# Cross-attention with four key sets on one core: keys copied at the slot's opening, last output and value products interleaved, a new end

## The chip, the core and the metric

The kernel runs on one core of one Trainium2 chip, written for that core's engines: TensorE (PE in the profile; its weight loads are listed apart as PEld), VectorE (DVE), ScalarE (ACT), GpSimd (POOL) and SyncE (SP), which here only issues DMAs. Each engine runs its own instructions in order and waits on semaphores for what other engines or DMAs produce. The metric is the device time of one execution in microseconds, median of several runs.

## The reference

The inputs `x` (32 x 512 x 640) and `ctx` (32 x 77 x 1024) are float32. For each of the 32 batches:

```python
q = heads(x @ to_q_w)                       # 20 heads of 32
k, v = heads(ctx @ to_k_w), heads(ctx @ to_v_w)
p = softmax(q @ k.T / sqrt(32))             # 512 x 77 per head
out = merge(p @ v) @ to_out_w + to_out_b + x
```

The source has four key sets (text, object, others, image prompt), but the context has exactly the 77 text tokens, so the other three sets are empty and add nothing.

## The kernel before, in words

All products are made in a float32 split: an operand is held as a rounded high part (type fp32r, written by ACT) and the remainder as a low part (written by DVE or POOL), and each product is three matmuls, high x high, high x low, low x high (`PAIRS`).

**Key and value phase (about the first 270 us).** The 2464 context rows are five groups of 512 (the last 416). For a group, `context` transposes the context on DVE (L167) and splits it (L103 on ACT, L104 on DVE); `keys` and `values_of_chunk` multiply it by the key and value weights on PE (L191, tiles `pk` and `pv`); `split_keys` and `split_values` split the results and write them to DRAM (`k_dram`, `v_dram`). `split_values` begins with a DVE transpose (L228) into one of two buffers `vs`, which must wait until the DMAs that read that buffer have landed. At the end of group 0 the order on DVE and ACT is: value split 2, key split 3, value split 3, context pieces 1 and 2 of the next group, key split 4, context pieces 3 to 7, value split 4. At the end of group 3 it is value split 3, then context pieces 1 to 7 of group 4, then value split 4.

**Slots.** After that the program is 160 slots, `slot(n)` with `b, j = divmod(n, 5)`: one batch and one of its five chunks of four heads. A slot's work is a pipeline over several slots, written out by hand, and the order of the calls is the order on each engine:

- queries of the next slot: 15 matmuls (L444, `pq<-xt,wq_s`), in two parts of 6 and 9; `split_q` copies and splits them (ACT L455, POOL L459, DVE L461).
- scores of this slot in four parts of 128 rows: 3 matmuls each (L479, `sc<-kb,qt`), into one of three PSUM buffers; DVE takes the row maxima (L487, `nm`) and ACT the exponentials (L497, `pn`, with row sums).
- probabilities of the slot before: reciprocal (DVE L507), multiplication (POOL L512, `normalize`), transposition (DVE L519, tile `z`) and four DMAs to DRAM (L526). They are loaded again (L535, L536, tile `raw`) and used four slots after their scores (`LAG`).
- probabilities taken now: `cast_p` (ACT L543) writes the high part, `rest_p` the last rows' high part (ACT L549) and the low part (DVE L550), `last_p` the last rows' low part (POOL L557).
- `values`: 6 matmuls (L571, `pa<-pp,vb`). `sum_a` adds the two halves (ACT L582, DVE L584), and in the next slot's opening `high_a` and `low_a` split the sum into `at` (ACT L591, DVE L596). `pa` has one buffer, so the next `values` waits for both.
- output product, `piece`: 24 matmuls per slot (L614, `po<-wo_s,at`), of one or two batches before; `finish` adds bias and residual (DVE L643) and stores. At j = 4 the first piece is 2 x 3 matmuls that need the `at` of the chunk just split.
- keys: `kb0` holds chunks 0 to 2 of a batch, `kb1` chunks 3 and 4. SP loads them (L420), at j = 3 for the next batch's `kb0` and at j = 0 for `kb1`, and `copy_keys` (POOL L424, L425) copies them into two further planes. It stands after `split_q` and `add_bias` of the slots j = 1 (`kb1`) and j = 4 (`kb0`), and the scores of the next slot, j = 0, read `kb0`.
- x of the next batch but one is loaded, transposed on DVE (L257, `TRANSPOSE_X` says in which of three places of which slot), and split (ACT L264, POOL L265) in slots j = 2 and 3.
- `add_bias` (POOL L607) adds the bias to the residual.

Slots 0 to 7 have no output product yet. `end()` takes the last four slots' probabilities and makes the remaining output products.

SP issues all DMAs of the slots in order, and a DMA waits until the one eight before it has landed.

The lines that the change moves most:

```python
            split_q(n + 1)
            if bias_now:
                add_bias(b - BIAS[j][0], BIAS[j][1])
            if j == 1:
                copy_keys(1)
            elif j == 4:
                copy_keys(0)
            exps(n, 2, *s)
```

Of the kernel before, what the change touches and what calls it, by code (L numbers as in the profile page):

```python
# [8 lines left out]
F32 = mybir.dt.float32  # L9
# [14 lines left out]
P = 128  # L24
# [27 lines left out]
def kernel(  # L52
# [278 lines left out]
    for g in range(LAST):  # L331
        for j in range(NC_):
            if g or j > 2:
                values_of(g, j, psk)
            if not g and j < 3:
                split_keys(0, j)
            if not g and j == 2:
                continue
            if j == 1:
                context(g + 1, 0)  # L340
            if not g and j == 3:
                split_values(0, 2)
                split_keys(0, 3)
            if j == NC_ - 1:
                if not g:
                    context(g + 1, 1, 2)
                    split_keys(0, 4)
                context(g + 1, *range(1 if g else 3, NK))
                if g + 1 == LAST:
                    kvw.release()  # L350
                    kvc.release()
                    xpool.append(
                        ctx.enter_context(
                            tc.tile_pool(name="xpool", bufs=1, reuse_waits="tile")
                        )
                    )
                    load_x(0)
            split_values(g, j, (None, split_wq, split_wo, None)[g])
# [180 lines left out]
    def cast_p(n):  # L539

        raw = raws[n]
        pp = late[0].tile([P, 5, S], FPR, tag="pp", name="pp", bufs=1)
        nc.scalar.copy(pp[:, 0:2, :], raw[:, 0:2, :])  # L543
        pps[n] = pp

    def rest_p(n):

        raw, pp = raws[n], pps[n]
        nc.scalar.copy(pp[:64, 4, :], raw[:64, 2, :])  # L549
        nc.vector.tensor_tensor(  # L550
            pp[:, 2:4, :], raw[:, 0:2, :], pp[:, 0:2, :].bitcast(F32), ALU.subtract
        )
# [9 lines left out]

    PASSES = [(p, 0, p + c) for p in range(2) for c in (0, 2)] + [(p, 1, 4) for p in range(2)]

    def values(n):
        b, j = divmod(n, NC_)
        g = GROUP_OF[j]
        pp, vb = pps.pop(n), vbs[g][:, j - GROUPS[g][0]]
        pas[n] = late[1].tile([P, 2, S], F32, tag="pa", name="pa", bufs=1)
        for m, (p, t, c) in enumerate(PASSES):  # L570
            nc.tensor.matmul(  # L571
# [39 lines left out]

    def project(b, t, h, j):
        for m, (a, c) in enumerate(PAIRS):
            nc.tensor.matmul(  # L614
# [4 lines left out]
                stop=(j == NC_ - 1 and m == 2),  # L619
            )  # L620


# [37 lines left out]
    BIAS = {2: (1, 0), 4: (1, 1), 0: (2, 2), 1: (2, 3)}  # L660
    TRANSPOSE_X = {0: ((), (), (0,)), 1: ((), (1,), (2,)), 2: ((3,), (), ())}
    SPLIT_X = {2: ((0,), (1,)), 3: ((2, 3), (4,))}
# [25 lines left out]
    def slot(n, beside=()):  # L688
# [9 lines left out]
        if not filling:  # L698
            refill(b, j, 0)
        if taken is not None:  # L700
            cast_p(taken)
# [39 lines left out]
        if not ahead:  # L741
            exps(n, 2, *s)
            piece(bo_, first)
            finish()
            s = scores(n, 3)
        early = ahead and has_out and j in (1, 4)
        if early:
            piece(bo_, first)
            finish()
        if not ahead:  # L750
            transpose_p(n - 1)
        if ahead:
            split_q(n + 1)
            if bias_now:
                add_bias(b - BIAS[j][0], BIAS[j][1])
            if j == 1:
                copy_keys(1)
            elif j == 4:
                copy_keys(0)
            exps(n, 2, *s)  # L760
        if n and not has_out:
            transpose_p(n - 1)
        if j == 4 and b + 2 < B:
# [3 lines left out]
        if not ahead:  # L767
            exps(n, 3, *s)
            normalize(n, sums(n))
            finish()  # L770
            piece(bo_, first + 1)
            values(taken)
            sum_a(taken)
# [4 lines left out]
        else:  # L778
            s = scores(n, 3)
        if taken is not None:  # L780
            values(taken)
# [20 lines left out]
    def end():  # L802
# [6 lines left out]
        piece(last - 1, 4)  # L809
        finish()  # L810
        high_a(N - 5)
        cast_p(N - 4)
        low_a(N - 5)
        rest_p(N - 4)
        last_p(N - 4)
        add_bias(last - 1, 2)
        piece(last - 1, 5)
        transpose_p(N - 1)
        add_bias(last - 1, 3)
        load_p(N - 2)  # L820
        piece(last - 1, 6)
        finish()
        take(N - 4)
        piece(last - 1, 7)
        cast_p(N - 3)
        rest_p(N - 3)
        last_p(N - 3)
        finish()
        load_p(N - 1)
        load_residual(last, 0)  # L830
        load_residual(last, 1)
        piece(last - 1, 8)
        take(N - 3)
        piece(last - 1, 9)
        cast_p(N - 2)
        rest_p(N - 2)
        last_p(N - 2)
        finish()
# [19 lines left out]

        begin(0, 0, 2)
        begin(1, 0, 2)  # L860
        take(N - 2)
        cast_p(N - 1)
        rest_p(N - 1)
        last_p(N - 1)
        for t in (0, 1, 3, 2):
            add_bias(last, t)
        begin(2, 0, 3)
        begin(0, 2, 4)
        begin(1, 2, 4)
        begin(2, 3, 4)  # L870
        begin(3, 0, 4)
        take(N - 1)
        begin(4, 0, 4)
        begin(5, 0, 4)

# [78 lines left out]
```

## Time and profile before

| | |
|---|---|
| median of 3 runs | 2061.75 us (2060.82 to 2064.63) |
| profiled execution, its own time | 2063.8 us |
| span of its instructions | 2062.0 us |
| TensorE busy | 1938.3 us, 94% |
| VectorE, ScalarE, GpSimd busy | 1571.7, 1551.5, 1368.4 us |
| mean granted TensorE clock | 0.981 |
| DMA | 431 MB, mean 209 GB/s |

The page gives for each engine the busy time and instructions, then the span in slices, the DMA queues, the chain of work that ended last, and the costliest groups of instructions by source line, with the idle time of the engine before them and what ended it. A matmul's end is modelled and overlaps the next one's start, so what a group of matmuls costs is read from start to start. Times in the trace's views are from the span's start. The clock is shown as a share: 1.00 is full, 0.50 half.

The slots are regular. From the start of one slot's first scores to the next one's, slots j = 0 to 4 take about 10.1, 9.9, 10.3, 10.2 and 13.4 us; the slot j = 0 takes 11.7 us in 13 of the batches.

### The profile page before, as it was taken

To read this page: it belongs to the slowest core of one execution; us is meant where nothing else is said; L and a number is where in the kernel's file an instruction comes from. 1 tells how busy PE (TensorE), PEld (TensorE's weight loads), DVE (VectorE), ACT (ScalarE), POOL (GpSimd) and SP (SyncE) were. 2 spreads that over 40 slices of the span, in tenths; PEclk is the share of its full clock that TensorE was granted. 3 is DMA by queue.
4 is the path that set the end of the run, shared out by engine and by line. 5 is a ranking of instruction groups with operands and counts; after the bars stand their busy time and mean duration, and the time that the engine had idled before them with its cause. 6 is when DMAs were issued, how large, how long until landed. Compare 5 with 4: busy or idle time off the path is not lost.

```text
span 2062.0 us, 37523 instructions
## 1 busy us (share of the span) xinstructions
PE 1938.3 (94%) x10332; PEld 1690.2 (82%) x10332; DVE 1571.7 (76%) x2494; ACT 1551.5 (75%) x6210; POOL 1368.4 (66%) x1116
## 2 busy tenths in 40 slices
PE   9999997999999999999999999999999999999997
PEld 7787886888888888888888888888888888888887
DVE  4344457888888888888888888888888888888874
ACT  3232258888888888888888888888888888888872
POOL 1000166777777777877777777777777777877763
PEclk9999998999999999999999999999999999999999
DMA  9878778888888888878788888878788888888774
GB/s 194 199 180 229 178 187 222 218 217 221 208 214 219 207 218 217 221 208 222 198 215 211 218 209 210 223 214 224 206 219 212 214 219 210 219 216 211 202 198 143
DMA packets 565023, 431.37 MB, mean 209 GB/s; under 512 B 191120, under 2 KB 473168, under 8 KB 564816
## 3 DMA queue, kind: packets, MB, share of 16 engines
q1 hardware_dynamic: 560304, 414.47, 79.2%
q0 software_dynamic: 4416, 14.34, 2.1%
q8 instruction: 85, 1.39, 0.3%
q14 instruction: 122, 1.00, 0.2%
q10 hardware_dynamic: 96, 0.16, 0.0%
HBM read 247.17 MB, written 181.64 MB: 208 GB/s over the span
## 4 chain that ended last, share of the span: by engine, by line
DVE 35%; PE 17%; issue 14%; ACT 12%; DMA 9%; POOL 6%; SPq 6%; DVEq 0%; POOLq 0%; ACTq 0%
DVE z L519 8%; ACT pn L497 7%; DVE nm L487 5%; PE pq L444 5%; DVE pp L550 5%; DVE qt L461 5%; DMA raw<-pd 4%; DVE pa L584 3%; DVE xs L257 3%; PE po L614 3%; DMA xs<-in_x_dram 3%; PE sc L479 2%; DVE at L596 2%; PE pk L191 2%; PE pv L191 2%
## 5 line engine op out<-in xcount | busy, mean ns | idle before, releaser
L497 ACT ACTIVATE pn<-sc,nm 128x77 f32<-128x77 f32 x2560 | 802.7, 334 | 137.4 <-DVE nm L487 130.3
L614 PE MATMUL po<-wo_s,at 128*128 128x320 f32 x3840 | 641.0, 315 | 35.2 <-DVE at L596 28.4
L444 PE MATMUL pq<-xt,wq_s 128*128 128x512 f32 x2400 | 647.6, 410 | 3.5 <-POOL xt L265 0.3
L614 PEld LDWEIGHTS po<-wo_s,at 128*128 128x128 f32 x3840 | 571.8, 190 | 46.1 <-DVE at L596 37.1
L557 POOL TENSOR_TENSOR pp<-raw,pp 64x512 fp32r<-64x512 f32 x160 | 304.6, 1904 | 369.3 <-ACT pp L549 301.2
L497 ACT ACTIVATION_READ_ACCUMULATOR pn<-sc,nm 128x1 f32 x2560 | 541.5, 212 | 0.0
L444 PEld LDWEIGHTS pq<-xt,wq_s 128*128 128x128 f32 x2400 | 438.5, 195 | 93.5 <-POOL xt L265 16.6
L479 PEld LDWEIGHTS sc<-kb,qt 128*128 128x128 f32 x1920 | 337.4, 192 | 133.5 <-POOL kb L425 62.3
L479 PE MATMUL sc<-kb,qt 128*128 128x154 f32 (+1 forms) x1920 | 342.1, 281 | 66.4 <-POOL kb L425 48.7
L487 DVE TENSOR_REDUCE nm<-sc 128x4 f32<-128x308 f32 x640 | 291.5, 464 | 136.5 <-PE sc L479 132.3
L512 POOL TENSOR_TENSOR pn<-pn,rs 128x1232 f32<-128x1232 f32 x160 | 364.2, 2277 | 14.2 <-DVE rs L507 1.8
L461 DVE TENSOR_TENSOR qt<-pq,qt 64x512 fp32r<-64x512 f32 x320 | 220.2, 688 | 122.6 <-ACT qt L455 117.6
L571 PE MATMUL pa<-pp,vb 128*128 128x512 f32 x960 | 256.5, 402 | 5.2 <-DVE at L596 2.4
L519 DVE STREAM_TRANSPOSE z<-pn 128x1280 f32<-128x1280 f32 x160 | 241.8, 1512 | 6.1 <-POOL pn L512 0.8
L584 DVE TENSOR_TENSOR pa<-pa,aw 64x512 f32<-64x512 f32 x320 | 222.7, 696 | 28.1 <-ACT aw L582 17.7
L550 DVE TENSOR_TENSOR pp<-raw,pp 128x1024 fp32r<-128x1024 f32 x160 | 202.5, 1266 | 29.7 <-ACT pp L543 29.7
L265 POOL TENSOR_TENSOR xt<-xs,xt 128x512 fp32r<-128x512 f32 x160 | 202.6, 1292 | 33.6 <-ACT xt L264 30.8
L459 POOL CAST qt<-qt 64x512 fp32r<-64x512 f32 x320 | 195.4, 611 | 33.1 <-ACT qt L455 14.3
L582 ACT COPY aw<-pa 64x1024 f32<-64x1024 f32 x160 | 162.0, 1013 | 65.9 <-PE pa L571 62.9
L571 PEld LDWEIGHTS pa<-pp,vb 128*128 128x128 f32 x960 | 173.8, 189 | 43.3 <-DVE at L596 11.9
L607 POOL TENSOR_TENSOR xr<-xr,bias 128x640 f32<-128x640 f32 x128 | 200.7, 1569 | 12.2 <-PE sc L479 2.0
L543 ACT CAST pp<-raw 128x1024 fp32r<-128x1024 f32 x160 | 168.9, 1056 | 1.8 <-DMA raw<-pd 1.8
(46 smaller groups left out, 1566.6 us busy)
## 6 DMA issues: line engine op xcount, KB each, us to landing
pd<-z SPq DMA_DIRECT2D x640, 160.0 KB, 3.2
raw<-pd SPq DMA_DIRECT2D x160, 512.0 KB, 4.1
xs<-in_x_dram SPq DMA_DIRECT2D x128, 320.0 KB, 7.4
xr<-in_x_dram SPq DMA_DIRECT2D x128, 320.0 KB, 3.3
out_dram<-xr SPq DMA_DIRECT2D x127, 320.0 KB, 3.6
raw<-pd SPq DMA_DIRECT2D x160, 128.0 KB, 4.2
v_dram<-vs SPq DMA_DIRECT2D x80, 192.0 KB, 3.9
k_dram<-ks POOLq DMA_DIRECT2D x20, 512.0 KB, 3.2
```

Of the source, the lines that this page charges most:

```text
L444: nc.tensor.matmul(pqs[n], wq_s[:, k, a, j * P : (j + 1) * P], xts[b, k][:, c, :], start=(k == 0 and m == 0), stop=(k == NC_ - 1 and m == 2),)
L461: nc.vector.tensor_tensor(qt[r, 1 + w, :], pq[r], qt[r, 0, :].bitcast(F32), ALU.subtract)
L479: nc.tensor.matmul(sc[:, cols], qt[:, m, t * P : (t + 1) * P], keys_, start=(m == 0), stop=(m == 2),)
L487: nc.vector.tensor_reduce(nm, sc[:, :KCOLS].rearrange("p (h k) -> p h k", k=NKEY), AX.X, ALU.max, negate=True)
L497: nc.scalar.activation(pnb[n % 2][:, at, :NKEY], sc[:, i * NKEY : (i + 1) * NKEY], AF.Exp, bias=nm[:, i : i + 1], accum_out=sms[n][:, at : ...
L512: nc.gpsimd.tensor_tensor(pf, pf, rs.unsqueeze(2).to_broadcast([P, NQ * HPC, NKEY]), ALU.mult)
L519: nc.vector.transpose(z.rearrange("p b t j -> p t b j"), pn.rearrange("p (t h) k -> p t (h k)", t=NQ).rearrange("p t (b i) -> p t b i", i=Q),)
L550: nc.vector.tensor_tensor(pp[:, 2:4, :], raw[:, 0:2, :], pp[:, 0:2, :].bitcast(F32), ALU.subtract)
L557: nc.gpsimd.tensor_tensor(pp[64:, 4, :], raw[:64, 2, :], pp[:64, 4, :].bitcast(F32), ALU.subtract)
L571: nc.tensor.matmul(pas[n][:, p, :], vb[:, p, t, :], pp[:, c, :], start=(c == p), stop=(t == 1),)
L584: nc.vector.tensor_tensor(pa[64 * p : 64 * p + 64, 0], pa[:64, p], aw[:, p], ALU.add)
L614: nc.tensor.matmul(pos[b, t, h][:, :HALF], ats[b * NC_ + j][:, a, t * P : (t + 1) * P], wos[0][:, j, c, h * HALF : (h + 1) * HALF], start= ...
```

## The change

- `split_values` of chunk 3 in the key and value phase stands after context pieces 1 and 2 of the next group.
- `copy_keys` stands at the opening of the slots j = 1 and j = 4, ahead of `cast_p`.
- The copy of the probabilities' last rows (ACT L549) moves from `rest_p` into `cast_p`: it runs ahead of `high_a`.
- `values` makes its six products in another order (both halves' first product, then both second, then both third) and can be made in two parts. `close_first`, at j = 4, replaces the first piece and `values`: 2 x 2 output matmuls that need only the high part of `at`, four of the values' matmuls, 2 x 1 output matmuls that need the low part, the last two of the values' matmuls.
- One transposition of x in slot j = 1 moves from behind the slot's third scores to behind its second exponentials.
- In the slots without output, the transposition of the probabilities stands behind the fourth scores.
- `end()` has a new order: in each step `turn` sums and splits one slot's values alternately with the cast of the next one's probabilities, and the output products of the last batch are made in layers (chunks 0 and 1 of four tiles, then chunk 2, then chunk 3).

The same amount of every kind of instruction is executed, apart from the last slots' order.

```diff
             if not g and j == 3:
                 split_values(0, 2)
                 split_keys(0, 3)
+            if j == 3:
+                continue
             if j == NC_ - 1:
+                context(g + 1, 1, 2)
                 if not g:
-                    context(g + 1, 1, 2)
                     split_keys(0, 4)
-                context(g + 1, *range(1 if g else 3, NK))
+                split_values(g, 3, (None, split_wq, split_wo, None)[g])
+                context(g + 1, *range(3, NK))
...
         nc.scalar.copy(pp[:, 0:2, :], raw[:, 0:2, :])
+        nc.scalar.copy(pp[:64, 4, :], raw[:64, 2, :])
         pps[n] = pp
 
     def rest_p(n):
 
         raw, pp = raws[n], pps[n]
-        nc.scalar.copy(pp[:64, 4, :], raw[:64, 2, :])
...
-    PASSES = [(p, 0, p + c) for p in range(2) for c in (0, 2)] + [(p, 1, 4) for p in range(2)]
+    PASSES = [(p, 0, p + c) for c in (0, 2) for p in range(2)] + [(p, 1, 4) for p in range(2)]
...
+    def close_first(b, n):
+
+        for m0, m1, v0, v1 in ((0, 2, 0, 4), (2, 3, 4, 6)):
+            for h in range(2):
+                project(b, 0, h, NC_ - 1, m0, m1)
+            values(n, v0, v1)
+        closed.extend(((b, 0, 0), (b, 0, 1)))
...
-    TRANSPOSE_X = {0: ((), (), (0,)), 1: ((), (1,), (2,)), 2: ((3,), (), ())}
+    TRANSPOSE_X = {0: ((), (), (0,)), 1: ((1,), (), (2,)), 2: ((3,), (), ())}
...
         if not filling:
             refill(b, j, 0)
+        if j == 1:
+            copy_keys(1)
+        elif j == 4 and more:
+            copy_keys(0)
         if taken is not None:
             cast_p(taken)
...
         if early:
-            piece(bo_, first)
+            if j == 4:
+                close_first(bo_, taken)
+            else:
+                piece(bo_, first)
             finish()
...
-            if j == 1:
-                copy_keys(1)
-            elif j == 4:
-                copy_keys(0)
             exps(n, 2, *s)
-        if n and not has_out:
-            transpose_p(n - 1)
...
         else:
             s = scores(n, 3)
-        if taken is not None:
+            if n:
+                transpose_p(n - 1)
+        if taken is not None and not (early and j == 4):
             values(taken)
...
+        def turn(n):
+            sum_a(n)
+            cast_p(n + 1)
+            high_a(n)
+            rest_p(n + 1)
+            low_a(n)
+            last_p(n + 1)
...
-        begin(0, 0, 2)
-        begin(1, 0, 2)
-        take(N - 2)
-        cast_p(N - 1)
-        rest_p(N - 1)
-        last_p(N - 1)
+        for i in range(4):
+            begin(i, 0, 2)
+        values(N - 2)
+        turn(N - 2)
         for t in (0, 1, 3, 2):
             add_bias(last, t)
-        begin(2, 0, 3)
-        begin(0, 2, 4)
-        begin(1, 2, 4)
-        begin(2, 3, 4)
-        begin(3, 0, 4)
+        for i in range(4):
+            begin(i, 2, 3)
+        for i in (4, 5):
+            begin(i, 0, 3)
         take(N - 1)
-        begin(4, 0, 4)
-        begin(5, 0, 4)
+        for i in range(6):
+            begin(i, 3, 4)
```

More of the change, by code (lines that the diff above doesn't have):

```diff
@@ L559, in last_p, with values @@
         )
-    PASSES = [(p, 0, p + c) for p in range(2) for c in (0, 2)] + [(p, 1, 4) for p in range(2)]
-    def values(n):
+    PASSES = [(p, 0, p + c) for c in (0, 2) for p in range(2)] + [(p, 1, 4) for p in range(2)]
+    def values(n, m0=0, m1=6):
         b, j = divmod(n, NC_)
         g = GROUP_OF[j]
-        pp, vb = pps.pop(n), vbs[g][:, j - GROUPS[g][0]]
-        pas[n] = late[1].tile([P, 2, S], F32, tag="pa", name="pa", bufs=1)
-        for m, (p, t, c) in enumerate(PASSES):
+        pp, vb = pps[n], vbs[g][:, j - GROUPS[g][0]]
+        if m1 == 6:
+            pps.pop(n)
+        if m0 == 0:
+            pas[n] = late[1].tile([P, 2, S], F32, tag="pa", name="pa", bufs=1)
+        for p, t, c in PASSES[m0:m1]:
             nc.tensor.matmul(
@@ L610, in output_bank, with project @@
         pos[b, t, h] = late[1].tile([P, S], F32, tag="po", name="po", bufs=2)
-    def project(b, t, h, j):
-        for m, (a, c) in enumerate(PAIRS):
+    def project(b, t, h, j, m0=0, m1=3):
+        for m in range(m0, m1):
+            a, c = PAIRS[m]
             nc.tensor.matmul(
@@ L747, in slot @@
         if early:
-            piece(bo_, first)
+            if j == 4:
+                close_first(bo_, taken)
+            else:
+                piece(bo_, first)
             finish()
@@ L769, in slot @@
             normalize(n, sums(n))
+            piece(bo_, first + 1)
             finish()
-            piece(bo_, first + 1)
-            values(taken)
             sum_a(taken)
@@ L810, in end @@
         finish()
+        cast_p(N - 4)
         high_a(N - 5)
-        cast_p(N - 4)
+        rest_p(N - 4)
+        transpose_p(N - 1)
         low_a(N - 5)
-        rest_p(N - 4)
         last_p(N - 4)
         add_bias(last - 1, 2)
-        piece(last - 1, 5)
-        transpose_p(N - 1)
         add_bias(last - 1, 3)
         load_p(N - 2)
+        piece(last - 1, 5)
         piece(last - 1, 6)
         finish()
-        take(N - 4)
+        values(N - 4)
         piece(last - 1, 7)
-        cast_p(N - 3)
-        rest_p(N - 3)
-        last_p(N - 3)
         finish()
+        def turn(n):
[5 more added lines that the diff above has]
+            last_p(n + 1)
+        turn(N - 4)
         load_p(N - 1)
@@ L832, in end @@
         piece(last - 1, 8)
-        take(N - 3)
+        finish()
+        values(N - 3)
         piece(last - 1, 9)
-        cast_p(N - 2)
-        rest_p(N - 2)
-        last_p(N - 2)
+        turn(N - 3)
         finish()
```

## The prediction

> **What bounds the kernel now.** First the page: PE is busy 94% of the span, so the time is PE's work plus its waits. Then PE's waits by releaser, which name three places the change touches.
>
> ```profile
> PE 1938.3 (94%) x10332; PEld 1690.2 (82%) x10332; DVE 1571.7 (76%) x2494; ACT 1551.5 (75%) x6210; POOL 1368.4 (66%) x1116
> ```
>
> ```profile
> PE sc L479 <- POOL kb L425: 48.7, 29, 3.4
> PE po L614 <- DVE at L596: 28.4, 33, 1.1
> PE pk L191 <- ACT ct L103: 6.2, 2, 3.2
> ```
>
> Third, the timeline, for the end of a slot j = 4: PE waits 0.92 us for the low part of `at`, and 1.66 us at the next slot's first scores for POOL's key copies, which stand behind the bias addition.
>
> ```profile
> 1187.07 0.85 PE L614 MATMUL po<-wo_s,at 128*128 128x320 f32 x4 [0.92 <-DVE at L596]
> ...
> 1193.99 0.97 PE L479 MATMUL sc<-kb,qt 128*128 128x308 f32 x3 [1.66 <-POOL kb L425]
> 1194.76 2.85 PE L444 MATMUL pq<-xt,wq_s 128*128 128x512 f32 x6
> ```
>
> ```profile
> 1191.22 1.56 POOL L607 TENSOR_TENSOR xr<-xr,bias 128x640 f32<-128x640 f32 x1
> 1192.74 0.56 POOL L424 CAST kb<-kb 64x462 fp32r<-64x462 f32 x1
> 1193.36 0.57 POOL L425 CAST kb<-kb 64x462 fp32r<-64x462 f32 x1
> ```
>
> Fourth, stretches: after such a wait the granted clock (PEclk, behind POOL's count) is 0.50, so six matmuls take 2.85 us instead of 1.59. A slot j = 4 is 13.45 us with PE busy 10.76, one j = 1 is 9.86 us without idle time; DMA is full in j = 4 (share 1.02).
>
> ```profile
> 1194.60:1197.40 2.80, 2.80 (x7) 2.23 (x8) 2.32 (x4) 2.08 (x10) 1.98 (x1) 0.50 1.12 318
> ```
>
> ```profile
> 1126.63:1140.08 13.45, 10.76 (x59) 8.81 (x58) 11.66 (x18) 13.01 (x50) 11.53 (x11) 1.00 1.02 232
> ...
> 1150.19:1160.05 9.86, 9.86 (x59) 8.93 (x58) 8.60 (x16) 8.09 (x34) 6.05 (x5) 1.00 0.75 194
> ```
>
> Last, the chain of waits. It doesn't run through PE here, but from transposition to transposition through DVE and ACT without a gap: this is what comes next once PE's waits go.
>
> ```profile
> 1312.54 1.50 DVE z L519
> ...
> 1319.23 1.34 ACT pn L497 x8
> 1320.57 0.48 ACT qt L455
> ...
> 1321.08 0.69 DVE qt L461
> ...
> 1324.54 0.73 DVE xs L257
> ...
> 1344.35 1.52 DVE z L519
> ```
>
> **The steady part.** From the opening of slot 9 (361.7 us) to that of slot 154 (1945.1) are 29 batches, 54.60 us each. Five slots at the 9.85 of j = 1 make 49.25, the floor on PE. But each batch must also pass the DVE and ACT chain. In the batch at 1127 us, `z` starts at 1127.02 (j = 3), 1137.33, 1149.10, 1159.59, 1170.83, 1180.92: steps of 10.31, 11.77, 10.49, 11.24, 10.09, in sum 53.90. DVE waited for scores in the second, 0.57 and 1.72 us, and only there. Without these the chain needs 53.90 - 2.29 = 51.61. So of PE's 5.35 us over its floor, some 3 can go before this chain binds.
>
> *Copies at the opening.* With the copies ahead, the first scores of j = 0 start right behind the output product: 1.66 us of wait go, and with them the slow clock, 3.41 us at half speed = 1.7 us, in 12 of the 29 batches. This ends DVE's two waits: counted from the end of L596 in j = 4 (1133.11), PE would need 4.8 us to the scores (4 values 0.93, 2 po 0.30, 2 values 0.47, scores 0.33, 18 po 2.70) and reach the fourth scores of j = 0 at about 1145.7 instead of 1148.1, when DVE, 0.57 earlier, is ready at 1146.3. What is queued behind the copies on POOL: L557, the multiplication L512, the query copies L459, and so DVE's `z` and the next scores. The copies (2 x 0.57) fit between POOL's last L265 (ends 1130.82) and L557 (starts 1132.27). They wait for the key DMAs; the last lands 1.2 to 2.6 us before L265's end in every batch but the first. In j = 1 POOL idles 4.7 us there. The SP queue isn't reordered, but its DMAs follow `z` and so come earlier.
>
> *Interleaving.* The values' first product overwrites `pa`, which L596 reads, so it waits for the same L596; the cover grows from 2 to 4 output matmuls, 2 x 0.16 = 0.33 us of the 0.92. DVE's L643 comes about 0.6 us later; its engine idles 0.70 before L461, so no cost, taken as 0.
>
> *Last rows copied behind the cast.* L549 takes 0.62 us either way. In j = 0 to 2 it fills ACT's wait for DVE's L584 (0.42 to 1.13 us); POOL's L557 starts 0.9 to 1.7 us sooner. In j = 3 and 4 `at` ends 0.6 later, but still 0.2 before DVE comes to L596: 0.
>
> *x transposed earlier.* In j = 1 L257 (0.80 us) leaves the chain for the 1.10 us in which DVE waits for ACT's L455: 51.61 - 0.80 = 50.81.
>
> *What is new.* In j = 4 the copies run beside DVE's L550, which lies on the chain. L550 takes 1.20 us, but 1.52 in j = 3, where POOL's L265 was running when it began: between 0 and 0.32 us per batch; a gain is excluded, nothing gets shorter beside other work. I take 0.3, the nearest row. And `raw` lands only about 1 us before ACT's cast in j = 0, and in j = 1 the cast moves 2.3 us nearer to DMAs that queue in the full slot j = 4; DVE's L550 has 0.5 to 1.6 us of cover there: 0 to 0.5, taken 0.2. Together 51.3, a gain of 3.3 x 30 batches (29, and the one to slot 159) = **99 us**. Bounds: 50.8, and 52.4 (with 0.8 for a transposition that doesn't fit, 0.32 and 0.5).
>
> The Trainium skill, "GPSIMD Engine Reference", section 8, speaks against the earlier copies: POOL shares its SBUF interfaces with VectorE and contends with instructions of two SBUF inputs, which L550 is. By it every L550 beside POOL's work would lengthen; the trace shows 1.20 beside L557 (which itself goes from 1.27 to 2.1 us) and 1.52 only behind L265. Lengthening by 0.32 in four more slots would make the gain 60 us instead of 99.
>
> The same skill, "TensorE: Matmul & The Clock Gate", says the clock falls to half after an idle window of about 3.4 us. The row above shows it after a wait of 1.66 us. By the rule these waits wouldn't cost clock and the change nothing more than the waits; by the row the slow stretches go with them.
>
> **Key and value phase.** PE waits 3.17 + 0.22 us at 69.6 and 3.04 + 0.20 at 183.9, since the context pieces stand behind a value split whose buffer a DMA still reads. With restarts from start to start that is 3.8 + 3.7, and both are followed by 3.41 us of half clock, 1.7 each. Now piece 1 follows the key split (DVE free at 63.5) and is ready about 65.5, before PE needs it at 66.2; the value split has no one waiting. PE is full from there to 256 us: **-10.9 us**. If piece 3 became late (due 73.4, ready about 71.6): half of it.
>
> **Fill.** In slot 4 the last keys land at 317.28, after POOL's L265 (314.83). L557, behind them now, starts at 318.4 instead of 315.2; PE's first scores of slot 5 then follow the query copies at about 324.0 instead of 322.07: **+2 us** (0 to 4).
>
> **End.** From 1999.8 PE waits 9.2 us and runs 13.7 us at half clock (6.8 lost). In the new order `values` of the last four chunks follow L596 directly: one step is 6 values 1.4 us, ACT's sum copy 1.0 and DVE's L584 1.4, beside which ACT now casts the next chunk (1.1) and its last rows (0.6), then `at` 0.6 and L596 0.7, so some 6 us, with 12 to 30 output matmuls of 0.157 us ahead of the next values. Walked through with these, the sums start at about 2008.5, 2016.5, 2022.5, 2029.4 and 2035.6 instead of 2012.4, 2020.6, 2029.3, 2036.6 and 2047.0. Behind the last remain some 7 us of PE and 4 of stores: **-10 us** (-3 to -15).
>
> **Sum.** -99 - 10.9 + 2 - 10 = -118; span 2062.0 to 1944. The profiled execution took 2063.8, 1.8 over its span and 2.05 over the median; so the median should be **1944 to 1946; I say 1945**.
>
> **Rivals.**
> *A, PE alone counts* (the chain gives way): 49.65 per batch (0.4 for restarts, as j = 2 shows now: 10.27 against 9.85), 30 x 4.95 + 19 = 168, 1895 us. The 94% speaks for it, the gapless chain against. 5%.
> *B, the chain is tighter*: contention, late `raw`, or the transposition not fitting its gap (it leaves 0.25 us): 52.4, 30 x 2.2 + 19 = 85, 1977 us; further wins failing, up to 2040. DMA's full slot speaks for it. 16%.
> *C, slower: POOL stops at the opening.* If the key DMAs landed behind L265, L557, L512, the query copies and the next scores all stand behind them. L265's end is 2.3 us after landing and PE has 0.8 more; the gain per batch is 3.9 with the fixed parts. So it decides from 7.0 us later than now, against 2 to 3 us from issue to landing; at 9 us later, 30 x 2.0 over 2062 = 2122 us. Only the filling slot shows a late landing (2.45 us). 6%.
> *D, no change*: PE waits as long elsewhere; then DVE's chain would have to have no slack now, but it waits 2.29 us. 1%.
>
> The forecast case, 1918 to 1972, has 72%. The range 1918 to 1990 adds the nearer half of B and leaves out A, the farther half of B, C and D (20%). A measurement of this kernel tells about 0.2% (4 us) from no change; faster 0.93, same 0.01, slower 0.06.
>
> **What would show it.** `sc <- POOL kb L425` gone from PE's waits; `po <- DVE at` replaced by `pa <- DVE at` of 0.6 to 1.5 us in j = 4; batches of 51.3 us, all alike; almost no half clock between 340 and 1940; DVE's waits for scores gone in j = 0; L550 in j = 4 at 1.2 or 1.5; no wait at 69 and 183. Wrong if the slots j = 1 to 3 get longer than 10.3, or POOL waits for `kb` DMAs.

## The result and the profile after

The changed kernel takes 1941.5 us (median; 1939.5 to 1943.7) against 2062.8 for the kernel before on the same chip: a ratio of 0.941, 95% interval 0.940 to 0.943. The forecast was 1945. The profiled execution took 1943.7 us, its span is 1941.9. Line numbers have moved: L479 is now L482 (scores), L444 is L447 (queries), L425 is L428 (key copies), L591 and L596 are L597 and L602 (`at`), L549 is L547 (last rows), L550 is L553, L557 is L560, L614 is L621 (output), L571 is L577 (values), L461 and L455 are L464 and L458 (query split), L519 is L522 (`z`), L643 is L658, L487 and L497 are L490 (maxima) and L500 (exponentials), L543 is L546 (large cast), L582 and L584 are L588 and L590 (sum of the halves).

Two lines of the changed kernel's page, engines and granted clock:

```profile
PE 1893.9 (98%) x10332; PEld 1668.6 (86%) x10332; DVE 1568.0 (81%) x2494; ACT 1536.8 (79%) x6210; POOL 1391.0 (72%) x1116
...
PEclk9999998999999999999999999999999999999999
```

PE's waits by releaser (total, times, longest):

```profile
PE po L621 <- ACT at L597: 9.8, 32, 1.3
PE sc L482 <- POOL qt L462: 7.0, 8, 2.1
PE sc L482 <- ACT pn L500: 6.1, 3, 5.5
PE sc L482 <- DMA kb<-k_dram: 3.9, 2, 3.5
PE pa L577 <- DVE at L602: 3.0, 4, 1.2
```

And DVE's wait for the scores, before and after:

```profile
DVE nm L487 <- PE sc L479: 132.3, 111, 2.6
```

```profile
DVE nm L490 <- PE sc L482: 13.4, 7, 2.5
```

The wait for POOL's key copies, 48.7 us in 29 places, is gone, and of 28.4 us for the low part of `at` 9.8 are left, now for its high part. All half clock between slot 9 and slot 158 is gone: what is left of it lies at 266 us, at several places between 304 and 338 us, and behind 1891 us. PE is busy 98% of the span; the experiments show that its work is all the same not what sets the batch.

The place that the prediction shows, from the output products of j = 4 to the next batch, in PE's timeline of the changed kernel:

```profile
1026.79 0.86 PE L621 MATMUL po<-wo_s,at 128*128 128x320 f32 x4 [0.26 <-ACT at L597]
1027.77 1.19 PE L577 MATMUL pa<-pp,vb 128*128 128x512 f32 x4
...
1032.56 0.49 PE L482 MATMUL sc<-kb,qt 128*128 128x308 f32 x3
1032.89 1.58 PE L447 MATMUL pq<-xt,wq_s 128*128 128x512 f32 x6
```

The scores of j = 0 (1032.56) start behind the output products without a wait, and the six query products after them take 1.58 us instead of 2.85. What is left in j = 4 is a wait of 0.26 us for `at`, and matmuls that are drawn out because they start one by one as their operands come. From first scores to first scores this slot j = 4 takes 11.10 us and the next j = 0 9.83; the medians of the 29 batches are 11.33 and 9.83, and were 13.44 and 10.13. Two stretches that lie 0.2 to 0.3 us behind these starts show full clock (1.00) and full DMA engines (shares of 0.97 and 0.98):

```profile
1021.62:1032.90 11.28, 10.78 (x62) 9.12 (x60) 9.62 (x15) 11.00 (x45) 10.85 (x10) 1.00 0.97 246
1032.90:1042.70 9.80, 9.80 (x59) 8.91 (x58) 8.54 (x14) 8.98 (x41) 8.51 (x6) 1.00 0.98 266
```

By stages, from the starts of the slots' first scores in the two profiled executions:

| stage | before | after | difference | forecast |
|---|---|---|---|---|
| to slot 0 (key and value phase) | 272.9 | 264.6 | -8.3 | -10.9 |
| slots 0 to 8 (fill) | 89.6 | 94.2 | +4.7 | +2 |
| 29 batches, slots 9 to 153 | 1582.7 | 1476.9 | -105.8 | -96 |
| slots 154 to 157 | 44.8 | 40.7 | -4.2 | -3 |
| slot 158 to the end | 72.1 | 65.5 | -6.5 | -10 |
| span | 2062.0 | 1941.9 | -120.1 | -118 |

A batch takes 50.93 us instead of 54.58; forecast were 51.3.

### The profile page after: what moved, and what is told of

Same layout as the page of the kernel before. It is cut to its first block, busy times and chain, and to the rows that moved or that the text cites. A ratio compares the mean times of both kernels' runs of the same rounds, so it can differ in the third digit from the quotient of the medians.

```text
span 1941.9 us, 37554 instructions
## 1 busy us (share of the span) xinstructions
PE 1893.9 (98%) x10332; PEld 1668.6 (86%) x10332; DVE 1568.0 (81%) x2494; ACT 1536.8 (79%) x6210; POOL 1391.0 (72%) x1116
## 5 line engine op out<-in xcount | busy, mean ns | idle before, releaser
L500 ACT ACTIVATE pn<-sc,nm 128x77 f32<-128x77 f32 x2560 | 802.0, 335 | 129.3 <-DVE nm L490 121.4
L621 PE MATMUL po<-wo_s,at 128*128 128x320 f32 x3840 | 637.6, 314 | 10.8 <-ACT at L597 9.8
L447 PE MATMUL pq<-xt,wq_s 128*128 128x512 f32 x2400 | 630.5, 402 | 3.3 <-POOL xt L265 0.2
L621 PEld LDWEIGHTS po<-wo_s,at 128*128 128x128 f32 x3840 | 571.3, 189 | 21.4 <-ACT at L597 15.2
L500 ACT ACTIVATION_READ_ACCUMULATOR pn<-sc,nm 128x1 f32 x2560 | 546.9, 214 | 0.0
L447 PEld LDWEIGHTS pq<-xt,wq_s 128*128 128x128 f32 x2400 | 428.1, 190 | 89.2 <-POOL xt L265 16.2
L482 PEld LDWEIGHTS sc<-kb,qt 128*128 128x128 f32 x1920 | 329.4, 189 | 69.0 <-POOL qt L462 13.9
L560 POOL TENSOR_TENSOR pp<-raw,pp 64x512 fp32r<-64x512 f32 x160 | 290.6, 1816 | 131.2 <-ACT pp L547 112.8
L482 PE MATMUL sc<-kb,qt 128*128 128x154 f32 (+1 forms) x1920 | 323.4, 275 | 18.7 <-POOL qt L462 7.0
L464 DVE TENSOR_TENSOR qt<-pq,qt 64x512 fp32r<-64x512 f32 x320 | 220.2, 688 | 111.4 <-ACT qt L458 106.4
L490 DVE TENSOR_REDUCE nm<-sc 128x4 f32<-128x308 f32 x640 | 291.2, 459 | 19.8 <-PE sc L482 13.4
L577 PE MATMUL pa<-pp,vb 128*128 128x512 f32 x960 | 263.3, 404 | 8.1 <-DVE at L602 3.0
L522 DVE STREAM_TRANSPOSE z<-pn 128x1280 f32<-128x1280 f32 x160 | 241.8, 1511 | 8.6 <-DMA pd<-z 2.5
L590 DVE TENSOR_TENSOR pa<-pa,aw 64x512 f32<-64x512 f32 x320 | 222.5, 695 | 19.3 <-ACT aw L588 8.9
L553 DVE TENSOR_TENSOR pp<-raw,pp 128x1024 fp32r<-128x1024 f32 x160 | 203.7, 1273 | 32.6 <-ACT pp L546 32.4
L265 POOL TENSOR_TENSOR xt<-xs,xt 128x512 fp32r<-128x512 f32 x160 | 202.5, 1291 | 33.5 <-ACT xt L264 30.8
L462 POOL CAST qt<-qt 64x512 fp32r<-64x512 f32 x320 | 194.9, 609 | 31.9 <-ACT qt L458 14.1
L577 PEld LDWEIGHTS pa<-pp,vb 128*128 128x128 f32 x960 | 171.9, 189 | 46.7 <-DVE at L602 15.1
L546 ACT CAST pp<-raw 128x1024 fp32r<-128x1024 f32 x160 | 168.7, 1055 | 42.7 <-DMA raw<-pd 40.9
L588 ACT COPY aw<-pa 64x1024 f32<-64x1024 f32 x160 | 161.9, 1012 | 20.1 <-PE pa L577 16.0
```

Source lines behind the costliest of these rows:

```text
L447: nc.tensor.matmul(pqs[n], wq_s[:, k, a, j * P : (j + 1) * P], xts[b, k][:, c, :], start=(k == 0 and m == 0), stop=(k == NC_ - 1 and m == 2),)
L464: nc.vector.tensor_tensor(qt[r, 1 + w, :], pq[r], qt[r, 0, :].bitcast(F32), ALU.subtract)
L482: nc.tensor.matmul(sc[:, cols], qt[:, m, t * P : (t + 1) * P], keys_, start=(m == 0), stop=(m == 2),)
L490: nc.vector.tensor_reduce(nm, sc[:, :KCOLS].rearrange("p (h k) -> p h k", k=NKEY), AX.X, ALU.max, negate=True)
L500: nc.scalar.activation(pnb[n % 2][:, at, :NKEY], sc[:, i * NKEY : (i + 1) * NKEY], AF.Exp, bias=nm[:, i : i + 1], accum_out=sms[n][:, at : ...
L522: nc.vector.transpose(z.rearrange("p b t j -> p t b j"), pn.rearrange("p (t h) k -> p t (h k)", t=NQ).rearrange("p t (b i) -> p t b i", i=Q),)
```

## The experiments

The theory to be tested is the forecast's: with PE's waits gone, a chain through DVE and ACT sets the batch. The rivals are that TensorE's own work and waits set it, and that each part is worth just the wait that it removes. "Per batch" is always the distance of slot 9 to slot 154 over 29 in the run's profile, so it comes from one execution. The four executions of a kernel lie 2 to 7 us apart (11 in one case), up to some 0.2 us per batch if all of it lay there; smaller differences are not read.

### The key copies alone

The kernel before, with this edit:

```diff
+        if j == 1:
+            copy_keys(1)
+        elif j == 4 and more:
+            copy_keys(0)
         if taken is not None:
             cast_p(taken)
...
-            if j == 1:
-                copy_keys(1)
-            elif j == 4:
-                copy_keys(0)
             exps(n, 2, *s)
```

> The kernel before, with the key copies alone moved to the slot's opening. Theory (TensorE's wait for the copies and the half clock behind it go, and then the chain through DVE and ACT binds at 51.6 us plus 0.2 to 0.5 of contention and late loads): 51.8 to 52.1 us per batch instead of 54.6, no half clock in the steady part, 1984 us (1978 to 1992). Rival 1 (the copies remove their own wait and clock and nothing else, 1.66 + 12/29 x 1.7 = 2.4 us per batch): 52.2 us, 1991 us. Rival 2 (the copies only move the wait to another place, and the interleaving is what gains): over 53.5 us per batch, over 2030 us.

Measured: 1984.9 us, ratio 0.961 (0.959 to 0.964), 51.80 us per batch. PE's largest wait is then the old one for the low part of `at`, 0.9 us in each j = 4 (line numbers of the kernel before):

```profile
PE po L614 <- DVE at L596: 27.8, 32, 1.0
```

So the copies alone give 2.78 of the 3.65 us per batch, more than their own wait and clock (2.4, rival 1's 1991 us), and land near the forecast's chain (51.6 and a little). PE is not quite off the path there: DVE still waits 0.34 us per batch for the scores of j = 0. Rival 2 falls: little of the gain is the interleaving's.

### The key copies back at their old place

The same lines the other way round, in the changed kernel.

> The changed kernel with the key copies at their old place behind the query split and the bias addition. Theory (the copies carry most of the steady gain, since every batch then again waits for them in TensorE, and DVE behind it): the wait of the first scores of j = 0 for the copies is back with 1.5 us or more, half clock is back, 53.5 to 54.2 us per batch, 2020 to 2040 us. Rival (the transposition, the interleaving and the last rows' copy have taken so much off DVE and ACT that the copies would no longer be late): under 52 us per batch, under 1975 us.

Measured: 2044.5 us, ratio 0.990 (0.988 to 0.993), 54.33 us per batch, a little beyond the theory's end. PE's waits and one place in its timeline:

```profile
PE sc L482 <- POOL kb L428: 53.8, 27, 3.2
```

```profile
1021.98 0.75 PE L482 MATMUL sc<-kb,qt 128*128 128x308 f32 x3 [1.95 <-POOL kb L428]
1022.57 2.28 PE L447 MATMUL pq<-xt,wq_s 128*128 128x512 f32 x6
```

The copies are worth 2.78 us per batch when they are moved first and 3.41 when moved last: without them the other parts leave 54.33 us of 54.58. They do shorten their slots: j = 2 and j = 3 by 0.41 and 0.37 us, and j = 4 by 0.49 with the wait at its end left out. But PE then stands at the copies for 1.95 us instead of 1.65, and half clock follows in 26 of the 29 batches instead of 12, which makes j = 0 longer by 0.74 us in the mean. Of the 1.27 us gained, 0.30 go into the longer wait and 0.74 into the clock. A wait that comes last hides what is gained before it, and here the clock behind it took more than the wait.

### The transposition of x back

```diff
-    TRANSPOSE_X = {..., 1: ((1,), (), (2,)), ...}
+    TRANSPOSE_X = {..., 1: ((), (1,), (2,)), ...}
```

> The changed kernel with the transposition of x in j = 1 back behind the third scores. Theory (the chain through DVE and ACT binds in every slot, and this transposition of 0.80 us lies on it in j = 1): 0.8 us more per batch, 51.7 us, 1965 us. Rival 1 (TensorE binds, which the 98% on the page and a slot j = 1 without TensorE waits speak for; the chain only has to be ready in j = 4, where DVE and ACT have caught up): 0 to 0.2 us per batch, 1942 to 1948 us.

Measured: 1960.8 us, ratio 0.950 (0.948 to 0.952), 51.50 us per batch, 0.58 more. That is less than the theory's 0.8 and well over rival 1's 0.2. PE uses this block of x only slots later, and in j = 1 it does not wait in either kernel; the time is lost in the next slot, j = 2, which gets 0.6 us longer and where PE now waits for DVE (the line below; 0.23 us per batch of it in j = 2). This is the strongest single sign of the chain: 0.80 us put on DVE between `z` and the addition L590 cost 0.58.

```profile
PE pa L577 <- DVE at L602: 10.1, 25, 1.3
```

### The interleaving back

```diff
-            if j == 4:
-                close_first(bo_, taken)
-            else:
-                piece(bo_, first)
+            piece(bo_, first)
...
-        if taken is not None and not (early and j == 4):
+        if taken is not None:
             values(taken)
```

with the old order of `PASSES`.

> The changed kernel with the first output piece of j = 4 and the values one after the other and the values' products in their old order. Theory by the forecast's terms (the interleaving only covers two more output matmuls, 0.33 us): 0.3 us more per batch, 1951 us. Rival 1 (the wait of j = 4 is TensorE's only one and so all of it counts: the output products would start behind the low part of at, at 1027.8 instead of 1026.8 in the batch at 1020 us): 0.9 to 1.0 us more per batch, 1970 us. Rival 2 (the chain through DVE and ACT binds, and TensorE's wait in j = 4 is only its slack): 0 us, 1942 us.

Measured: 51.27 us per batch in the profile, 0.35 more. The profiled execution, 1956.7 us, was the slowest of its four; the median is 1948.1 us, ratio 0.944 (0.941 to 0.947), so by the whole program's time alone rival 2 (no change) is not excluded. The trace excludes it: in each of the 29 batches DVE waits for the scores of j = 0, 0.34 us in the mean, where the changed kernel has no such wait. The forecast's 0.33 is met; rival 1, that the whole wait counts, would have been three times that.

### The last rows' copy behind `high_a` in j = 4, and in all slots

In j = 4 alone the `if` names the slot; the second kernel has it in every slot:

```diff
     def cast_p(n):
...
-        nc.scalar.copy(pp[:64, 4, :], raw[:64, 2, :])
+        if (n + LAG) % NC_ != 4 or n + LAG >= N:
+            nc.scalar.copy(pp[:64, 4, :], raw[:64, 2, :])
...
     def rest_p(n):
+        if (n + LAG) % NC_ == 4 and n + LAG < N:
+            nc.scalar.copy(pp[:64, 4, :], raw[:64, 2, :])
```

> The changed kernel with the copy of the probabilities' last rows behind the split of the sum again, in the slots j = 4 alone. Theory (ACT runs without a gap from the query copy of j = 3 to the high part of at in j = 4, and TensorE's first output products there wait for it; so the 0.62 us copy ahead of it is on the path, against the forecast's term of 0): 0.3 to 0.6 us less per batch, 50.3 to 50.6 us, 1924 to 1933 us. Rival 1 (the low part of at on DVE, for which the values wait 0.13 us right after, or POOL's last rows, then half a microsecond later, take the wait over): 0 to 0.15 us less, 1937 to 1942 us. Rival 2 (POOL's later last rows hold up the values' last products): slower, 0.3 us more per batch, 1951 us.

> The changed kernel with the copy of the probabilities' last rows behind the split of the sum in all slots, as before the change. Theory (in j = 0 to 2 the copy ahead fills ACT's wait for the sum, so putting it back there costs ACT up to 0.6 us, and in j = 4 it gains): between the run with j = 4 alone and the changed kernel, 50.5 to 51.2 us per batch, 1930 to 1950 us. Rival (the place of this copy in j = 0 to 3 doesn't count): the same as with j = 4 alone, to 0.1 us per batch.

Measured: 1942.4 us (ratio 0.941, 0.939 to 0.943) and 1940.6 (0.940, 0.939 to 0.942); 51.00 and 50.92 us per batch. Both are no change, against the theory of the first, and its rival 1 tells why. With the high part of `at` 0.6 us sooner in j = 4, PE's wait there only passes to the next engine: 0.62 us per batch for DVE in place of 0.26 for ACT and 0.13 for DVE (the line is of the first kernel; L580 and L605 are its values and low part of `at`):

```profile
PE pa L580 <- DVE at L605: 22.2, 35, 1.2
```

DVE makes that low part behind the probabilities' low part (L553 in the changed kernel), and this waits for ACT's large cast, which the edit does not move.

### Less work for PE, for DVE, for ACT, and a better order in j = 4

Three kernels leave out work of one engine each, and a fourth has another order. The edits: one query product left out per slot; half of DVE's residual additions left out; the last block of x not split in j = 3 (the block before it is used in its place); and in j = 4 `high_a` ahead of `cast_p`, `rest_p` behind the second scores.

```diff
             for m, (a, c) in enumerate(PAIRS):
+                if n > 9 and k == 0 and m == 1:
+                    continue
```

> The changed kernel without one of the 15 query products of every slot from 10 on (the high x low product of the first block of rows is left out of q), 0.25 us of TensorE per slot. Theory (the chain through DVE and ACT sets the batch of 50.9 us, TensorE only catches up to it): 50.7 to 50.9 us per batch, 1936 to 1942 us, and TensorE's waits grow by 1.2 us per batch. Rival (TensorE's work sets the batch, with a fixed wait in j = 4): 1.26 us less per batch, 49.7 us, 1904 us.

```diff
+            if h or not 2 <= b < B - 2:
                 nc.vector.tensor_tensor(
                     xr[:, cols], pos.pop((b, t, h))[:, :HALF], xr[:, cols], ALU.add
                 )
```

> The changed kernel without DVE's addition of the residual to the first half of each output row block, for all batches but the first two and the last two (4 of 8 instructions L658 per batch, 0.45 us each, 1.8 us of DVE per batch). Theory (the chain binds and passes through DVE in most slots): 0.4 to 1.2 us less per batch, down to 49.7, 1906 to 1930 us. Rival 1 (TensorE or ACT alone binds): 0 to 0.1 us less, 1938 to 1942 us.

```diff
         for c in xsplits[1]:
-            split_x(b + 1, c)
+            if 2 <= b < B - 2 and c == 4:
+                xts[b + 1, 4] = xts[b + 1, 3]
+            else:
+                split_x(b + 1, c)
```

> The changed kernel without the split of the last block of x in j = 3, from the third batch to the third from the end: the queries use the block before it in its place. This leaves out 0.62 us of ACT and 1.26 us of GpSimd per batch. Theory (what binds at 50.9 us is ACT's work from the middle of j = 3 to the opening of j = 0, where it has nothing but two waits of 0.17 us, and the alternation of DVE and ACT in the slots before): 0.4 to 0.6 us less per batch, 50.3 to 50.5 us, 1924 to 1930 us. Rival 1 (ACT is level with another bound, such as the loads of the probabilities, for which ACT waits 0.8 us in j = 1): 0 to 0.1 us, 1938 to 1942 us. Rival 2 (TensorE, whose query products wait 0.3 us for this block): 0.3 us, 1932 us, with ACT waiting more.

```diff
+        sooner = ahead and has_out and j == 4
+        if sooner:
+            high_a(takes[n - 1])
         if taken is not None:
             cast_p(taken)
-        if n - 1 in takes:
+        if n - 1 in takes and not sooner:
             high_a(takes[n - 1])
...
-        if taken is not None:
+        if taken is not None and not sooner:
             rest_p(taken)
         rs = sums(n - 1) if n else None
         if taken is not None:
+            raw = raws[taken]
             last_p(taken)
...
         s = scores(n, 1)
+        if sooner:
+            raws[taken] = raw
+            rest_p(taken)
+            raws.pop(taken)
```

> The changed kernel with another order in j = 4: ACT splits the high part of at ahead of the cast of the probabilities, and DVE makes the low part of at and the second row maxima ahead of the probabilities' low part. TensorE's two waits in j = 4 should go in every theory. Theory (the chain through DVE and ACT sets the batch, and TensorE's 1.2 us in j = 4 are slack that it only displays): the second exponentials come 0.17 us sooner, 0.1 to 0.3 us less per batch, 50.6 to 50.8 us, 1933 to 1938 us, and TensorE waits in other places instead. Rival (TensorE's wait in j = 4 is on the path): 1.0 to 1.3 us less per batch, 49.7 to 49.9 us, 1904 to 1911 us.

| kernel | us | ratio (95%) | per batch |
|---|---|---|---|
| changed kernel | 1941.5 | 0.941 (0.940 to 0.943) | 50.93 |
| less for PE | 1943.2 | 0.942 (0.940 to 0.943) | 50.94 |
| less for DVE | 1941.2 | 0.941 (0.940 to 0.942) | 50.89 |
| less for ACT (and POOL) | 1935.6 | 0.938 (0.937 to 0.939) | 50.62 |
| `high_a` first in j = 4 | 1939.3 | 0.940 (0.938 to 0.941) | 50.96 |

TensorE's work does not bind: 1.26 us of it less per batch gave nothing. Its listed waits grew by 0.50 us per batch, not by the 1.2 that the theory expected; its busy time fell by only 0.51, so the rest went into matmuls drawn out. Nor does its wait in j = 4 set the batch: in the last kernel PE's wait for the high part of `at` is 1.9 us in the whole run instead of 9.8, and the batch is the same. The 0.1 to 0.3 us that the theory had expected there are not seen either.

```profile
PE po L621 <- ACT at L597: 1.9, 2, 1.3
```

Half of DVE's residual additions (1.8 us per batch) gave nothing either, against the theory's expectation. The waits say why: DVE now waits 0.37 us longer for ACT's query copy in j = 0 and as much in j = 1 (1.47 and 0.74 us, against 1.10 and 0.37), 0.31 us for ACT's cast in j = 3, where it hardly waited, and 0.3 more in j = 4. What was left out stood in front of places where DVE waits for ACT. The theory took every DVE instruction for a part of the chain; these were not.

ACT's 0.62 us (and POOL's 1.26) gave 0.30, half of it and less than the theory's 0.4 to 0.6. PE's listed waits are then down to 0.10 us per batch, from 0.31, which fits that PE stands next to the chain; this run does not show what took the other half.

### All four together

> The four edits before, which alone gave 0.0 (a query product left out of each slot), 0.04 (half of the residual additions left out), 0.30 (the last block of x not split) and 0.0 us per batch (the high part of at first in j = 4), all together. It leaves out the same work as those. Theory (TensorE, DVE and ACT are level to within some 0.3 us at 50.9 us per batch, so that each one cut alone meets the next): together they give clearly more than the sum of 0.34, 50.0 to 50.3 us per batch, 1914 to 1924 us. Rival (one further bound that none of the four touches, the loads of the probabilities in the full slots j = 4 and j = 0, holds the batch): 50.55 to 50.65 us, 1932 to 1936 us, and ACT's wait for these loads in j = 1 grows from 0.8 us to 2 us or more.

Measured: 1937.0 us, ratio 0.938 (0.936 to 0.940), 50.59 us per batch: the rival's number and not the theory's. But the rival's reason does not hold. ACT's wait for the loads of the probabilities in j = 1 is 1.2 us per batch, not 2 or more, and over the whole run it is less than in the kernel with less for ACT alone (the first line is of that kernel, the second of all four):

```profile
ACT pp L546 <- DMA raw<-pd: 70.7, 65, 3.1
```

```profile
ACT pp L548 <- DMA raw<-pd: 60.5, 54, 2.4
```

What holds the batch can be followed in the changed kernel's timeline, back towards the batch before: at each instruction to what released it, or to the one before it on its engine. DVE, slot j = 2:

```profile
999.37 1.41 DVE L464 TENSOR_TENSOR qt<-pq,qt 64x512 fp32r<-64x512 f32 x2 [0.37 <-ACT qt L458]
1000.80 0.48 DVE L490 TENSOR_REDUCE nm<-sc 128x4 f32<-128x308 f32 x1
1001.32 1.51 DVE L522 STREAM_TRANSPOSE z<-pn 128x1280 f32<-128x1280 f32 x1
1002.86 1.42 DVE L590 TENSOR_TENSOR pa<-pa,aw 64x512 f32<-64x512 f32 x2
1004.19 0.83 DVE L257 STREAM_TRANSPOSE xs<-xs 128x640 f32<-128x640 f32 x1
1004.95 0.43 DVE L490 TENSOR_REDUCE nm<-sc 128x4 f32<-128x308 f32 x1
1005.31 0.47 DVE L658 TENSOR_TENSOR xr<-po,xr 128x320 f32<-128x320 f32 x1
1005.71 1.20 DVE L553 TENSOR_TENSOR pp<-raw,pp 128x1024 fp32r<-128x1024 f32 x1
1006.84 0.24 DVE L510 RECIPROCAL rs<-sm 128x16 f32<-128x16 f32 x1
1007.00 0.62 DVE L602 TENSOR_TENSOR at<-pa,at 128x512 fp32r<-128x512 f32 x1
1007.54 0.46 DVE L490 TENSOR_REDUCE nm<-sc 128x4 f32<-128x308 f32 x1
...
1009.88 1.41 DVE L464 TENSOR_TENSOR qt<-pq,qt 64x512 fp32r<-64x512 f32 x2 [0.76 <-ACT qt L458]
```

From 999.37 to 1008.00 DVE has no gap. Then ACT takes over: its exponentials start at 1008.04, 1.28 us after ACT had become free, when the maxima of 1007.54 are there; then its query copy, which releases DVE at 1009.88. In j = 0 and 1 the chain goes the same way. In j = 3 it stays on ACT, which runs from 1017.82 to the cast in j = 4, for which DVE waits:

```profile
1024.69 1.06 ACT L546 CAST pp<-raw 128x1024 fp32r<-128x1024 f32 x1
1025.63 0.63 ACT L547 CAST pp<-raw 64x512 fp32r<-64x512 f32 x1
```

```profile
1025.78 1.23 DVE L553 TENSOR_TENSOR pp<-raw,pp 128x1024 fp32r<-128x1024 f32 x1 [0.83 <-ACT pp L546]
```

In this batch no DMA is on the path. PE is level with it in j = 4: DVE waits 0.67 us for the output product (which had waited for ACT's `at`), and when that addition is done ACT's query copy has just come (1029.97). Followed back in the same way by the listed waits in 28 batches, a DMA of the probabilities ends a wait on the path in 4 of them. In the kernel with all four edits the path goes through DVE and ACT alone in 20 of the 28, and in the other 8 such a DMA ends a wait on it. None of the four edits takes anything from the j = 0 to 2 part of the path. So that this chain holds the batch rests on the transposition put back (+0.58), on ACT's share left out (-0.30), on the edits to PE (0), and on the timeline. No run shortened it in j = 0 to 2 of the changed kernel: how much could be gained there before PE or the loads hold the batch, and at which instruction, is not shown.

### Key copies at the old place in j = 1 and in the first j = 4

```diff
-        if j == 1:
-            copy_keys(1)
-        elif j == 4 and more:
+        if j == 4 and b and more:
             copy_keys(0)
...
+            if j == 1:
+                copy_keys(1)
+            elif n == 4:
+                copy_keys(0)
             exps(n, 2, *s)
```

> The changed kernel with two of the key copies at their old place: those of chunks 3 and 4 (in every slot j = 1) and those of the first slot j = 4. Theory (in the filling slots GpSimd stops at the opening for key DMAs that land late, 8.3 us in slot 6, as the slower rival said, and TensorE then waits 2.1 and 5.5 us; in the steady part the copies in j = 1 only cost what POOL has to spare): slots 4 to 8 take 53 us instead of 57.5, the batch stays at 50.8 to 51.0 us, 1937 us (1935 to 1940). Rival 1 (the fill has another cause): 57 us for the slots 4 to 8, 1941 us. Rival 2 (GpSimd's wait for the keys in j = 1, 1.7 us per batch, and the products L553 lengthened beside it do count in the steady part): 0.3 to 0.5 us less per batch, 1923 to 1930 us.

Measured: 1941.4 us, ratio 0.941 (0.940 to 0.942), 50.91 us per batch. In the steady part POOL's waits for the key DMAs in j = 1 cost nothing, as the theory said: rival 2 falls. In the fill POOL does stop as the slower rival of the forecast described, in one slot: at the opening of slot 6, for keys that land late.

```profile
332.52 0.44 POOL L427 CAST kb<-kb 64x308 fp32r<-64x308 f32 x1 [8.27 <-DMA kb<-k_dram]
```

```profile
334.42 0.97 PE L482 MATMUL sc<-kb,qt 128*128 128x308 f32 x3 [5.51 <-ACT pn L500]
```

But PE's wait of 5.51 us does not stand behind POOL. It ends with ACT's exponentials, these had waited for DVE's maxima (332.55), and DVE was held by a transposition of x whose load came late:

```profile
331.78 0.85 DVE L257 STREAM_TRANSPOSE xs<-xs 128x640 f32<-128x640 f32 x1 [1.81 <-DMA xs<-in_x_dram]
```

```profile
333.03 0.33 ACT L500 ACTIVATE pn<-sc,nm 128x77 f32<-128x77 f32 x1 [1.94 <-DVE nm L490]
```

With the copies at the old place there, slots 5 to 8 take 40.3 us instead of 45.6, but slot 4 takes 14.6 instead of 11.9, since its scores wait for the copies again. Slots 4 to 8 come to 54.9 us, where the theory had 53 and rival 1 (another cause) 57. The fill's whole gain is 2.3 us in the profiles, and the medians are equal, as rival 1 had it. Between the kernels with the copies at the opening the fill varies by more than that (90.6 to 98.4 us). So what the copies cost in the fill is not shown; several engines wait there for late loads.

## Why the prediction was right, and where its terms were off

*Copies at the opening.* Right: the wait, the half clock and DVE's waits for the scores go together, and a chain through DVE and ACT binds next. The forecast's number for it, 51.6 and 0.5 for what is new, was measured as 51.80 with the copies alone. The 51.61 rests on a reading that left something out: it took off two waits for the scores in the step of j = 0, 0.57 and 1.72 us. That step has a third:

```profile
1145.07 0.48 DVE L487 TENSOR_REDUCE nm<-sc 128x4 f32<-128x308 f32 x1 [1.10 <-PE sc L479]
```

Taken off too, it would have made the chain 50.5. Leaving it in came out right, because in the changed kernel DVE waits as long at this place, now for ACT's query copy; the forecast gave no reason, so this is luck:

```profile
1039.36 1.41 DVE L464 TENSOR_TENSOR qt<-pq,qt 64x512 fp32r<-64x512 f32 x2 [1.10 <-ACT qt L458]
```

*x transposed earlier.* Taken as 0.80 us, measured as 0.58.

*Interleaving.* Taken as 0.33 us of PE's wait; taken back, it cost 0.35 per batch. The size was right. It is no term of the 51.3, which took it as given that the scores of j = 0 no longer hold DVE up. Without the interleaving they do: DVE waits there 0.34 us for them, with the copies alone as with the interleaving taken back. The waits left in j = 4 were named as 0.6 to 1.5 us for DVE; they are 0.26 for ACT and 0.13 for DVE, with some 1 us more in matmuls that are drawn out (11.3 us for the slot, less these waits and the 9.85 of j = 1).

*Last rows copied behind the cast.* Taken as 0 in j = 3 and 4, with ACT's wait filled in j = 0 to 2; measured as 0 in all.

Taken one by one, the four parts are worth 2.78, 0.58, 0.35 and 0 us per batch, in sum 3.71, against 3.65 together.

*What is new.* The 0.3 us for the copies beside L550 was a mis-sized term: it is 0, and POOL pays in place of DVE. Beside the copies of j = 4 L553 takes 1.23 us, as L550 did there before, and the second copy is longer:

```profile
1025.98 1.46 POOL L428 CAST kb<-kb 64x462 fp32r<-64x462 f32 x1
```

instead of 0.57, at no cost. In j = 3, the row the 0.3 was taken from, the median of L553 fell from 1.51 to 1.23, while single batches of j = 1 and 2 got longer; over the run L553 is busy 203.7 us and L550 was 202.5. So the price that the forecast set against the earlier copies, 0.32 in four more slots, was not paid. The 0.2 for late `raw` can't be told apart: ACT waits 0.8 us per batch for it in j = 1, yet DVE has no gap there. With neither of the two the forecast's own rows give 50.81, near the 50.93 measured; its 51.3 was 0.37 too long, 11 us in 30 batches. But as the residual additions show, not every DVE instruction counted into that chain lies on the path, and the transposition of x gave 0.58 and not 0.80, so that 50.81 comes this near is in part chance.

*Key and value phase.* The waits at 69 and 183 us are gone with their clock. Of the 10.9 us, 2.6 are lost again at once: the first scores of slot 0 wait 3.55 us for the key DMA, where they waited 0.94 for POOL's copies. -10.9 + 2.6 is the -8.3 measured. The forecast asked what is late next inside this phase and not at its end.

*Fill.* The +2 for slot 4 did not come: slot 4 takes 11.9 us instead of 14.1. The +4.7 is made of +1.6 in slots 0 to 3, -2.2 in slot 4 and +5.3 in slots 5 to 8, which the forecast did not look at; late loads are seen there, but no run separates their causes. The forecast named POOL waiting for `kb` DMAs as what would make it wrong: POOL does, 54 us over the run, but outside the fill it costs nothing.

*End.* The five sums start 19.4, 28.3, 36.1, 44.0 and 50.1 us behind the scores of slot 158, where the forecast had 18.5, 26.5, 32.5, 39.4 and 45.6 (and before 22.4 to 57.0). Half clock came back twice, 3.4 us each: from 1891.1, ahead of the first sum, and from 1911.6, in the fourth step, which is 7.9 us instead of 6.9. The second and third step are 8.9 and 7.8 us instead of 8.0 and 6.0, and in them the values wait for the low part of `at` and for POOL's last rows:

```profile
1902.93 1.64 PE L577 MATMUL pa<-pp,vb 128*128 128x512 f32 x6 [0.80 <-DVE at L602]
1909.29 1.17 PE L577 MATMUL pa<-pp,vb 128*128 128x512 f32 x4 [1.20 <-DVE at L602]
1911.34 1.01 PE L577 MATMUL pa<-pp,vb 128*128 128x512 f32 x2 [0.88 <-POOL pp L560]
```

The forecast counted neither the clock nor these waits: its "some 6 us" per step went along DVE and ACT only.

So the sum was near, 118 against 120.1, because the steady part's 11 us too little and the smaller errors (2.6, 2.7, 3.5) were of opposite sign. The mechanism and the size of the steady part were forecast; that the whole came within 4 us of the measured time is in part luck.

## What to carry to other kernels

Take the wait that comes last first: the same edits beside it were worth a quarter of a microsecond per batch with the wait in place, where a longer wait and more half clock took the rest, and 0.87 without it. An engine that is busy 98% need not be the bound; leave a little of its work out and see. Before counting an instruction as part of a chain, look whether its engine waits right behind it: if so, it is free.

## What the runs showed of the hardware

- When POOL and DVE's L553, which reads two operands in SBUF, run beside each other for more than some 0.2 us, one of them is lengthened and the other not, and which one goes mostly by who started first. L428 of j = 4, which starts 0.2 us behind L553, ends 0.43 us after L553's end in every batch (1.46 us instead of 0.57). In the other direction, where POOL's L265 began 0.83 us or more ahead, L553 ends 1.08 to 1.09 us after it and takes 1.49 to 1.54 us. The Trainium skill, "SBUF — State Buffer", section "SBUF: two separate sides", says that the shared port pair is an exclusive lock, that the first to start has it for the whole instruction, and that the other fully blocks; these rows agree. One detail differs: POOL's L560, started up to 0.51 us ahead of L553 by the profile, still was the one that waited (2.4 to 2.9 us instead of 1.28), and only from 0.55 us ahead on it was L553. So the order of the starts in the profile is not quite the order in which the lock is taken.
- Before, a wait of PE of 1.62 to 1.66 us for the copies was followed by half clock in 12 of 29 batches; with the copies back, a wait of 1.93 to 1.96 us was in 26 of 29, and the six query products took 2.28 us instead of 1.58 in the one shown. In every run with the copies of j = 4 at the opening there is no such wait and no half clock between slot 9 and slot 158.
